# Two spectral attention layers on one core: sums and scalings that may run on ScalarE and GpSimd, an inverse transform written in runs of 16, second-layer statistics on ScalarE, and a new order of all units

## The chip, the cores and the metric

The kernel runs on one NeuronCore of a Trainium2 chip; the other cores hold nothing of it. The metric is the device time of one execution in microseconds (us), from the core's first instruction to its last. The core has TensorE (PE; its weight loads are shown apart as PEld), VectorE (DVE), ScalarE (ACT) and GpSimd (POOL); DMAs are issued from SyncE (SP) and ScalarE. SBUF is the on-chip memory, PSUM the memory that TensorE writes to.

## The reference

Two layers of the same form are applied to x of shape (2, 56, 128, 128), that is 2 batches of 56 images of 128 x 128. Cut to what matters, one layer is:

```python
def spectral_conv(x, w, b):              # 32 x 16 complex modes are kept
    xf = rfft2(x, norm='forward')
    top = einsum('bihw,iohw->bohw', xf[:, :, :16, :16], c(w[0]))
    bot = einsum('bihw,iohw->bohw', xf[:, :, -16:, :16], c(w[1]))
    ...
    return irfft2(of, s=(H, W), norm='forward') + b
def fno_layer(x, w, b, sw, sb, norm=False, act=False):
    y = spectral_conv(x, w, b)
    if norm: y = inorm(y)
    y = y + skip1x1(x, sw, sb)
    return gelu(y) if act else y
# layer, x: (2, 56, 128, 128)
xg = group_norm(x, 32)                   # groups over the last axis
xa = xg.reshape(112, 1, 128, 128); xn = inorm(xa)
k, q, v = (fno_layer(xn, ...) for each of K, Q, V)          # 8 heads each
attn = softmax(heads(q) @ heads(k).T * scale)               # 56 x 56 a head and batch
out = fno_layer(attn @ heads(v), P)
att = inorm(out + xa); an = inorm(att)
h = fno_layer(an, M0, norm=True, act=True)
h = fno_layer(h, M1, norm=True, act=False)
x = x + inorm(h) + att
```

## The kernel before

Everything is fp32. A batch's picture lies in SBUF as `X2[:, b]`, images on partitions (two halves of 64, 56 used) and 64 rows of 128 pixels along the free axis; it is worked on in 8 units of 128 x 1024, numbered n = 0 to 7. Transforms are matmuls with constant cosine and sine matrices, and only the 32 x 16 kept modes of an image are ever computed. The names of the steps stand in the code as functions, one call for each layer L and batch b:

- `turned`: transposes a unit on TensorE, copies it from PSUM to `P[b]`, and takes the sums for the group norm. Odd units do this on ScalarE with accumulating activations (a copy into `P`, then a square into `dump`); even units are copied and go through two `bn_stats` on VectorE.
- `modes_chain`, `gram`, `scores`, `values`, `softmax_chain`, `mix_chain`, `heads`, `norms_chain`: the group norm's scale, the forward transform, the attention in mode space, and the scale factors of all the instance norms. They are short dependent operations, mostly on VectorE; every inverse root (`root`) is one `pow` on GpSimd. `scale_x` multiplies the picture by the group norm's factor `gvr` in 16 pieces of 128 x 512, on GpSimd or VectorE.
- `gelu`, 8 units a batch: a unit's original picture is loaded from DRAM into one of three buffers `xr`; matmuls with the weights `BTx` mix the images into PSUM; VectorE reads that PSUM tile and `xr`, and writes their scaled sum to `X2` (the `scalar_tensor_tensor` X<-psum,scalars,xr); `synthesis` then adds the inverse transform to the same PSUM tile, which therefore has to wait for that read; ScalarE takes the gelu and a sum of squares, TensorE transposes and transforms the result.
- `h_chain`: the second transform's norms, short dependent operations again, ending with `inverse`, which makes `Z` by two VectorE transposes of 128 x 896 from PSUM.
- `end`, 8 units a batch: `synthesis` from `Z`, then P<-P,scalars,psum on VectorE, then the sum with `X2` (on GpSimd, on VectorE or, for odd units of layer 2, as a matmul with the identity), and a store to DRAM. In layer 1 the unit goes straight on to `turned` of layer 2.

In layer 1 batch 0 runs about 20 to 40 us ahead of batch 1, and layer 2 follows batch by batch. "Warm" matmuls (`psum<-xr,ones`) have no result that is used; 20 of them stand in the order.

All calls are recorded first as units (`Work`), each with the engines it may run on. `ORDER` then lists every unit by a step to its number and a letter for its engine (V VectorE, S ScalarE, G GpSimd, T TensorE, Q the SP queue), and `issue` gives them out in that order. `PLACES` names the PSUM bank of each tile. An engine does its instructions in the order in which they are issued; semaphores make it wait for others. All records of the trace carry the line of `issue`, so steps are told apart by tile names and shapes.

Of the kernel before, what the change touches and what calls it, by code (L numbers as in the profile page):

```python
# [11 lines left out]
ALU = mybir.AluOpType  # L12
# [9 lines left out]
11Q -2Q 17G 1G -17S -9Q -1S 2S 3S 23G 85G -78G 82V -1V -61T -16T -3V 15T -2T 1T 11T -19T 5T 10T -28G 89G -114Q 58S  # L22
-59Q 30G 5T 20S 6T -57S 112V 1G 1V 1T 2S -1S 3V -1S 10V -129Q 2Q 8Q -1Q 15G 38T -25T -3T 29S -6S -9T 11S -19T 81G -56T
-57Q 126V 3G 1G -10G -67V 5V 86V -145S 60V -7V 16T 75V -97V 23S -64S 56T 3T -2S 3S -20V 21V -6V 7V 79V -142Q 52S 7S
-45G 52S -43T 7T -4T 117V -109T -15T 16T 43T 66T -70T -69Q 66T 8S 45V -12G 15V 18V -24V 25G -71V -73Q 65T 86G -6V -75S
1S 81V -26T 2S 2S -3S 2S -132Q 156G -6T -81S -64S 111G -1G 62T 1S -29V 2V 1T 8T 1V -144V 140T 9T -3T -43V -6V 44V 1T
14V -134T 408S -369V 75V -76V 120G -1G -32V -2T 12S -104V 41G 68T -82V 79V -87T 1S 1V 76V 13T 1T -69G 12G -53V 359S
-255S -82T 1S -13S 123V -6G 227Q -304V -107V 197V -129T 4T -3V 1V 98T 1T 1T 49V -148V 2S 5V 27G 46T 3T 17T -178S 81S
81V 3S -77S 91T -16G 17V 97V -69T 3T 67V -73T -24V -17S 42V 3S -188T 258T -97T -194Q 9Q 442Q -256V 24T 17T -14T 70V
144Q -212S 580V -608V 41V -12T -85G 86T -87G 91T -3S 66G -96G -56G 662V -508V 510G -662G 157V -72T -30V 31T 3V -33T  # L30
32S -31S 39V 1S -227S 293T 1V 124S -122T -167G 70G 82V -88V 95G -17G -181G 697G -497T 1V -71T 79T -10V -61V 1T 63T 3T
-161V 87V 76V 9V -84S 8S 1T 7T 1T 1T 43T 1V -86V 109S -75S 68V -67T 1S 7T 1S -5T 73T 1S -68V 1V 1V 40T -88V 144G -43T
-63T 74S -23V -40T 62V -61S 1S 10S -22V 76T -11T 1V -43V -9V 55V -54V 62T 7V 15V -21T 1T 46T -169V 601V -599G 55T 67T
# [158 lines left out]
class Work:  # L192


    def __init__(self):
        self.units, self.open, self.note, self.taken = [], None, "", []
# [1017 lines left out]
```

## Time and profile before

| | |
|---|---|
| median of 3 runs | 419.46 us |
| lowest and highest run | 412.94 and 429.42 us |
| span of the profiled execution, first to last instruction | 416.2 us |
| instructions | 17307 |
| busy: PE, PEld, DVE, ACT, POOL | 350.4, 247.7, 310.3, 195.1, 200.1 us |

The profiled execution is a run of its own; no time is given around its span, which lies within the three timed runs and 0.8% under their median. A busy time counts the union of an engine's instructions, so TensorE's includes the warm matmuls.

### The profile page before, as it was taken

What the parts mean: (1) busy time and instruction counts of PE and PEld (TensorE: products, weight loads), DVE (VectorE), ACT (ScalarE), POOL (GpSimd) and SP (SyncE); (2) the same over time, 40 slices, a digit from 0 to 9 for tenths busy, and PEclk for the clock granted to TensorE, in tenths of its full rate; (3) what the DMA queues carried; (4) which work ended last, traced back from release to release, by engine and by line L of the source; (5) the groups of instructions that cost most, each with busy time, mean ns of one, the idle gap of its engine ahead of it and who ended that gap; (6) DMA issues with size and microseconds to landing.
All of it is one profiled execution on the core that took longest, in us unless ns stands there. A gap on an engine that the chain in (4) does not pass through costs nothing.

```text
span 416.2 us, 17307 instructions
## 1 busy us (share of the span) xinstructions
PE 350.4 (84%) x7812; PEld 247.7 (60%) x7812; DVE 310.3 (75%) x544; ACT 195.1 (47%) x307; POOL 200.1 (48%) x288
## 2 busy tenths in 40 slices
PE   6769969999759888498887999989899989899970
PEld 2435667688435576265774987858676544675440
DVE  1155898666768667997998799974898977489992
ACT  1246572333238762026698336832237877791000
POOL 4781095623999302215912589336487170013740
PEclk9898999989989999589968999999999998999995
DMA  6997831300014421133020101772245463300776
GB/s 205 226 246 137 189 89 27 49 3 5 3 44 114 92 76 41 30 99 96 3 70 23 48 27 46 182 219 66 60 123 157 113 157 89 91 4 24 236 239 212
DMA packets 15850, 41.19 MB, mean 99 GB/s; under 512 B 2432, under 2 KB 2816, under 8 KB 15744
## 3 DMA queue, kind: packets, MB, share of 16 engines
q1 hardware_dynamic: 8426, 21.52, 20.4%
q10 hardware_dynamic: 7350, 18.57, 16.2%
q8 instruction: 61, 1.00, 1.0%
q14 instruction: 13, 0.11, 0.1%
HBM read 25.40 MB, written 14.68 MB: 96 GB/s over the span
## 4 chain that ended last, share of the span: by engine, by line
PE 24%; DVE 22%; issue 5%; DMA 5%; ACT 4%; POOL 2%; ACTq 0%; SPq 0%; DVEq 0%; POOLq 0%
PE psum L222 24%; DVE P L222 9%; DVE X L222 3%; DMA xr<-store 3%; DVE WU L222 2%; ACT P L222 2%; DVE scalars L222 2%; DVE WB L222 1%; POOL X L222 1%; DMA store<-X 1%; DMA xr<-x 1%; ACT WB L222 1%; DVE stats L222 1%; ACT dump L222 1%; DVE vd L222 1%
## 5 line engine op out<-in xcount | busy, mean ns | idle before, releaser
L222 POOL TENSOR_TENSOR X<-X,gvr 128x512 f32<-128x512 f32 x47 | 61.0, 1324 | 33.1 <-DMA store<-X 17.1
L222 ACT COPY P<-psum 128x896 f32<-128x896 f32 (+5 forms) x47 | 34.4, 741 | 58.5 <-PE psum L222 53.1
L222 PE MATMUL psum<-C,P 56*128 56x56 f32 (+4 forms) x1124 | 50.1, 259 | 12.4 <-DVE X L222 10.5
L222 PE MATMUL psum<-P 128*56 128x56 f32 (+2 forms) x1600 | 56.9, 226 | 4.1 <-issue 4.0
L222 PEld LDWEIGHTS psum<-C,P 56*128 56x128 f32 (+4 forms) x1124 | 41.9, 166 | 27.9 <-DVE X L222 13.1
L222 POOL TENSOR_TENSOR scalars<-scalars 56x1 f32<-56x1 f32 (+2 forms) x24 | 14.8, 616 | 87.8 <-DVE scalars L222 87.8
L222 PEld LDWEIGHTS psum<-P 128*56 128x56 f32 (+1 forms) x1600 | 49.7, 136 | 8.6 <-issue 5.5
L222 DVE SCALAR_TENSOR_TENSOR X<-psum,scalars,xr 128x1024 f32<-128x1024 f32 x32 | 40.2, 1275 | 14.8 <-DMA xr<-store 4.9
L222 ACT ACTIVATE P<-psum,scalars 128x1024 f32<-128x1024 f32 x32 | 34.1, 1110 | 33.2 <-PE psum L222 33.1
L222 ACT ACTIVATE dump<-P 128x1024 fp8e4<-128x1024 f32 (+1 forms) x48 | 49.0, 1022 | 1.2 <-DVE X L222 0.5
L222 DVE SCALAR_TENSOR_TENSOR P<-P,scalars,psum 128x1024 f32<-128x1024 f32 x32 | 39.6, 1269 | 3.7 <-PE psum L222 3.7
L222 POOL TENSOR_TENSOR X<-P,X 128x512 f32<-128x512 f32 x25 | 33.5, 1367 | 16.2 <-DVE P L222 16.1
L222 PE MATMUL psum<-X,BTx 57*64 57x512 f32 x256 | 33.9, 624 | 1.2 <-DVE P L222 0.6
L222 PE MATMUL psum<-C,X 56*128 56x56 f32 x512 | 21.5, 232 | 8.6 <-DMA X<-x 7.1
L222 PEld LDWEIGHTS psum<-C,X 56*128 56x128 f32 x512 | 18.8, 144 | 15.1 <-DMA X<-x 8.1
L222 DVE STREAM_TRANSPOSE P<-psum 128x448 f32<-128x448 f32 (+1 forms) x24 | 23.8, 1002 | 4.9 <-PE psum L222 4.8
L222 PE MATMUL psum<-xr,ones 128*128 128x512 f32 x40 | 23.9, 742 | 2.2 <-POOL xr L222 1.9
L222 DVE COPY P<-psum 128x896 f32<-128x896 f32 (+4 forms) x25 | 21.2, 852 | 5.9 <-PE psum L222 5.5
L222 ACT ACTIVATE P<-psum 128x896 f32<-128x896 f32 x16 | 14.6, 912 | 20.0 <-PE psum L222 20.0
L222 PE MATMUL psum<-P,C 128*64 128x112 f32 (+2 forms) x200 | 19.3, 318 | 4.9 <-DVE P L222 4.4
L222 DVE BATCH_NORM_STATS2 stats<-P 128x6 f32<-128x448 f32 x32 | 18.4, 608 | 4.8 <-ACT P L222 4.7
L222 ACT COPY WB<-psum 128x896 f32<-128x896 f32 x21 | 18.8, 905 | 6.7 <-PE psum L222 6.2
(189 smaller groups left out, 654.3 us busy)
## 6 DMA issues: line engine op xcount, KB each, us to landing
X<-x SPq DMA_DIRECT2D x11, 448.0 KB
xr<-store SPq DMA_DIRECT2D x20, 224.0 KB
store<-X ACTq DMA_DIRECT2D x18, 224.0 KB
out<-P ACTq DMA_DIRECT2D x18, 224.0 KB
xr<-x SPq DMA_DIRECT2D x16, 224.0 KB
xr<-x ACTq DMA_DIRECT2D x16, 224.0 KB
store<-X SPq DMA_DIRECT2D x14, 224.0 KB
out<-P SPq DMA_DIRECT2D x14, 224.0 KB
```

The lines of the kernel that those rows point to most:

```text
L222: getattr(engines[letter], method)(*args, **kw)
```

## The change

Each recorded piece of work may now have alternatives: `either()`, `orelse()` and `decided()` bracket two or three ways to do it, and the order marks the units that are not issued with the letter X. The alternatives are:

- In `gelu`, the sum X<-psum,scalars,xr on VectorE, or a scaling from PSUM on ScalarE (X<-psum,scalars) and then a sum with `xr` on GpSimd (X<-X,xr, 128 x 1024). The order takes the second for 13 of 32 units.
- In `end`, as before; or P scaled on ScalarE (P<-P,scalars), summed with X on GpSimd (P<-P,X) ahead of the synthesis, and one VectorE sum with PSUM at the end; or, in layer 2, the sum with X by matmul. The order takes the second for 13 of 32 units and the matmul for 5 (8 before).
- In `prepare`, the tables WU and WT by tensor products on GpSimd or VectorE, or by small activations on ScalarE (one group of 16 of them is taken).
- Each warm matmul may be left out; 6 of 20 stay.

`inverse` turns its blocks into `Z` in runs of 16 neighbouring elements, where before each element went 64 elements (256 bytes) further; in return the weights that `synthesis` loads from `Z` lie 16 elements (64 bytes) apart, where before they were neighbours. The rows of the constant `gh` are reordered to match. In layer 2 all 8 units of `turned` take their sums on ScalarE; `bn_stats` and `bn_aggr` remain in layer 1. Engines, order and PSUM banks of all units are new.

```diff
 class Work:
+    def either(self):
+        self.groups.append([len(self.units)])
+    def orelse(self):
+        self.groups[-1].append(len(self.units))
+    def decided(self):
+        cuts = self.groups[-1] + [len(self.units)]
+        self.groups[-1] = [list(range(a, b)) for a, b in zip(cuts, cuts[1:])]
+    def left_out(self):
+        return self.letters.get(len(self.units)) == "X"
...
         for n, letter in order:
+            if letter == "X":
+                continue
...
 # _constants
-    v, r, a, e, c = j // 2, j % 2, idx // 8, idx // 2 % 4, idx % 2
+    v, r, a, e, c = j // 2, j % 2, idx // 4 % 4, idx % 4, idx // 16
...
 # build (and in the same way WT in prepare)
+                work.orelse()
+                for l0 in range(0, 16, 4):
+                    with work.unit():
+                        for l in range(l0, l0 + 4):
+                            S.activation(
+                                WUv[:, t0 : t0 + 4, :, 32 * h : 32 * h + 32]
+                                .rearrange("p t a (c l) -> p t a c l", c=2)[:, :, :, :, l],
+                                tcs[:, 0:16, t0 : t0 + 4].rearrange("p (a c) t -> p t a c", c=2),
+                                AF.Copy, scale=C["same"][:, 16 * h + l : 16 * h + l + 1],
+                            )
+                work.decided()
...
 # turned
-        if n % 2:
-            o = n - n % 2
+        if L == 1 or n % 2:
+            o = 2 * n if L == 1 else n - 1
...
 # inverse
-        Zv = Z.rearrange("p (h k) -> p h k", k=64)
+        Zv = Z.rearrange("p (c k q) -> p c k q", c=2, q=16)
...
-                Zv[:, :, i : i + 28].rearrange("p h i -> p i h"),
+                Zv[:, :, i : i + 28].rearrange("p c i q -> p i c q"),
...
 # modes_chain, L == 1
+            V.tensor_reduce(mv, totals.rearrange("p (n k) -> p k n", k=2), AX.X, ALU.add)
...
 # synthesis
-                    o = 64 * (8 * A + 2 * e)
+                    o = 4 * A + e
...
-                        lhsT=Z[32 * j : 32 * j + 32, o : o + N],
+                        lhsT=Z[32 * j : 32 * j + 32].rearrange("p (m q) -> p m q", q=16)[:, :, o],
...
 # gelu
+                work.either()
+                V.scalar_tensor_tensor(base, flat, cols[:, 1:2], xr[:, n % 3], ALU.mult, ALU.add)
+                work.orelse()
+                S.activation(base, flat, AF.Copy, scale=cols[:, 1:2])
+                tt("G", base, base, xr[:, n % 3], ALU.add)
+                work.decided()
...
 # end
+                S.activation(hold_[v], hold_[v], AF.Copy, scale=st["hs"])
+                tt("G", hold_[v], hold_[v], bases[v], ALU.add)
...
+                V.scalar_tensor_tensor(h3, h3, st["hs"], flat[v], ALU.mult, ALU.add)
+                m = 512 if L == 0 else 1024
+                for o in range(0, 1024, m):
+                    tt("GV", dst[:, o : o + m], h3[:, o : o + m], base[:, o : o + m], ALU.add)
+                V.tensor_tensor(dst, flat[v], h3, ALU.add)
+                k = opened[v]
+                if L == 0:
+                    work.groups.append([[first, first + 1, first + 2], [k, k + 1, first + 3]])
+                else:
+                    work.groups.append([[first, first + 1], [k, k + 1, first + 2], [k + 2, first]])
...
 # warm
+        work.either()
         p = bank()
         T.matmul(p, lhsT=ones, rhs=xr[:, 0, :512], start=True, stop=True)
+        work.orelse()
+        work.decided()
...
 ORDER = """
-11Q -2Q 17G 1G -17S -9Q -1S 2S 3S 23G 85G -78G 82V -1V -61T -16T -3V 15T -2T 1T 11T -19T 5T 10T -28G 89G -114Q 58S
+33G -22S 15V 2G 27T -4T -10X 15X -24G -3G -19Q 103V -104S 107G 1V 1G 1V -5V 6V 1V -121S 1Q 114G -113S 47X 12T 61T -60S
```

What the new order does is shown at three places. The first is TensorE at the end of batch 0's load: transposes of units (`C,X`), warm matmuls (`xr,ones`), and the matmul that sums the group norm's statistics (`scalars,C 128x2`). Before:

```order
L222 MATMUL psum_63<-C_64,X2_68 128x56 x16
L222 MATMUL psum_63<-xr_78,ones_80 128x512 x4
L222 MATMUL psum_63<-C_64,X2_68 128x56 x64
L222 MATMUL psum_63<-xr_78,ones_80 128x512 x6
L222 MATMUL psum_63<-C_64,X2_68 128x56 x16
L222 MATMUL psum_63<-scalars_81,C_64 128x2
L222 MATMUL psum_63<-C_64,X2_68 128x56 x48
L222 MATMUL psum_63<-stage_65,C_64 32x5x8 x32
L222 MATMUL psum_63<-C_64,scalars_81 1x32
```

With the change:

```order
L247 MATMUL psum_63<-C_64,X2_68 128x56 x80
L247 MATMUL psum_63<-xr_78,ones_80 128x512 x2
L247 MATMUL psum_63<-C_64,X2_68 128x56 x32
L247 MATMUL psum_63<-stage_65,C_64 32x5x8 x32
L247 MATMUL psum_63<-xr_78,ones_80 128x512
L247 MATMUL psum_63<-scalars_81,C_64 128x2
L247 MATMUL psum_63<-C_64,X2_68 128x56 x32
L247 MATMUL psum_63<-P0_69,fwg0_96 32x448 x16
L247 MATMUL psum_63<-C_64,scalars_81 1x32
```

One warm matmul stands ahead of the statistics' matmul where six stood, and the transform (`P,fwg`) follows with fewer transposes of batch 1 between.

The second place is VectorE where batch 0 of layer 1 goes over from `norms_chain` to `gelu`: the inverse's two transposes, the multiplications of batch 1's picture (`X<-X,gvr1`), and the first sums of `gelu` (X<-psum,scalars,xr). Before:

```order
L222 STREAM_TRANSPOSE P0_69<-psum_63 128x28x32 x2
L222 TENSOR_TENSOR X2_68<-X2_68,gvr1_100 128x512
L222 SCALAR_TENSOR_TENSOR X2_68<-psum_63,scalars_81,xr_78 128x1024 x2
L222 TENSOR_SCALAR vd1_101<-C_64,scalars_81 56x56
L222 TENSOR_TENSOR dcq0_98<-psum_63,P0_69 1x56
L222 TENSOR_SCALAR dcq0_98<-dcq0_98,der0_92 1x56
L222 TENSOR_TENSOR D0_84<-D0_84,psum_63 128x448
L222 STREAM_TRANSPOSE stage_65<-stage_65 128x128
L222 SCALAR_TENSOR_TENSOR X2_68<-psum_63,scalars_81,xr_78 128x1024
```

With the change:

```order
L247 TENSOR_TENSOR D0_84<-D0_84,psum_63 128x448
L247 TENSOR_TENSOR X2_68<-X2_68,gvr1_102 128x512
L247 COPY scalars_81<-psum_63 128x2
L247 STREAM_TRANSPOSE P0_69<-psum_63 128x28x2x16 x2
L247 SCALAR_TENSOR_TENSOR X2_68<-psum_63,scalars_81,xr_78 128x1024 x2
L247 TENSOR_TENSOR X2_68<-X2_68,gvr1_102 128x512 x2
L247 SCALAR_TENSOR_TENSOR vd1_103<-psum_63,C_64 56x56
L247 TENSOR_REDUCE scalars_81<-vd1_103 56x1
L247 TENSOR_SCALAR scalars_81<-scalars_81 56x1
```

The multiplication that stood between the transposes and the first two sums now stands ahead of the transposes, and two more follow the sums.

The third place is ScalarE in layer 2, where `gelu` goes over from batch 0 (`P0`) to batch 1 (`P1`): gelus (P<-psum,scalars), squares (into `dump`), copies for the transform (`WB`) and loads of `xr`. Before:

```order
L222 ACTIVATE P0_69<-psum_63,scalars_81 128x1024 x2
L222 DMA xr_78<-store_79 56x1024
L222 COPY WB_74<-psum_63 128x896
L222 ACTIVATE dump_75,scalars_81<-P0_69 128x1024
L222 COPY WB_74<-psum_63 128x896
L222 ACTIVATE P1_70<-psum_63,scalars_81 128x1024 x2
L222 DMA xr_78<-store_79 56x1024
L222 ACTIVATE dump_75,scalars_81<-P0_69 128x1024
L222 ACTIVATE P1_70<-psum_63,scalars_81 128x1024 x2
```

With the change:

```order
L247 DMA xr_78<-store_79 56x1024
L247 ACTIVATE dump_75,scalars_81<-P0_69 128x1024 x2
L247 COPY WB_74<-psum_63 128x896
L247 ACTIVATE dump_75,scalars_81<-P0_69 128x1024
L247 ACTIVATE X2_68<-psum_63,scalars_81 128x1024
L247 ACTIVATE dump_75,scalars_81<-P0_69 128x1024
L247 DMA xr_78<-store_79 56x1024
L247 ACTIVATE P1_70<-psum_63,scalars_81 128x1024 x2
L247 ACTIVATE X2_68<-psum_63,scalars_81 128x1024
L247 DMA xr_78<-store_79 56x1024
```

Two scalings of a unit's sum (X<-psum,scalars), of batch 1's units 1 and 3, now stand between ScalarE's gelus and squares, and where two copies stood, one stands.

## Rows read from the trace of the kernel before

**Rows 1.** The page: busy times; shares of the chain that ended last

```profile
PE 350.4 (84%) x7812; PEld 247.7 (60%) x7812; DVE 310.3 (75%) x544; ACT 195.1 (47%) x307; POOL 200.1 (48%) x288
...
PE 24%; DVE 22%; issue 5%; DMA 5%; ACT 4%; POOL 2%; ACTq 0%; SPq 0%; DVEq 0%; POOLq 0%
```

**Rows 2.** Stretches of 20 or 8 us: PE, PEld, DVE, ACT, POOL busy (x); PEclk; DMA

```profile
24.00:32.00 8.00, 4.18 (x68) 3.04 (x67) 4.20 (x8) 2.34 (x5) 5.72 (x18) 0.88 1.02 243
...
160.00:180.00 20.00, 13.36 (x119) 9.06 (x116) 17.13 (x46) 1.81 (x5) 5.76 (x10) 0.66 0.23 59
...
200.00:220.00 20.00, 16.32 (x430) 13.54 (x424) 18.59 (x27) 17.83 (x31) 8.89 (x7) 0.83 0.14 38
```

**Rows 3.** Timeline, 30 to 39 us: start us, us, instructions merged

```profile
30.87 6.68 PE L222 MATMUL psum<-xr,ones 128*128 128x512 f32 x12
...
35.68 0.16 DVE L222 SCALAR_TENSOR_TENSOR scalars<-scalars 128x2 f32<-128x2 f32 x1
...
38.12 0.38 PE L222 MATMUL psum<-scalars,C 128*128 128x2 f32 x2
```

**Rows 4.** Timeline, 110 to 120 us

```profile
110.32 6.34 DVE L222 TENSOR_TENSOR X<-X,gvr 128x512 f32<-128x512 f32 x1
...
110.89 4.94 POOL L222 TENSOR_TENSOR X<-X,gvr 128x512 f32<-128x512 f32 x4
...
119.10 2.09 PE L222 MATMUL psum<-C,P 32*128 32x128 f32 x32 [5.74 <-DVE X L222]
```

**Rows 5.** VectorE's groups by form: busy us, mean ns, idle before

```profile
L222 DVE SCALAR_TENSOR_TENSOR X<-psum,scalars,xr 128x1024 f32<-128x1024 f32 x32 | 40.2, 1275 | 14.8 <-DMA xr<-store 4.9 <-DMA xr<-x 4.1 <-ACT P L222 3.2
...
L222 DVE BATCH_NORM_STATS2 stats<-P 128x6 f32<-128x448 f32 x32 | 18.4, 608 | 4.8 <-ACT P L222 4.7
L222 DVE TENSOR_TENSOR X<-X,gvr 128x512 f32<-128x512 f32 x17 | 18.2, 1074 | 0.3 <-DMA xr<-x 0.3
L222 DVE STREAM_TRANSPOSE P<-psum 128x896 f32<-128x896 f32 x8 | 13.7, 1732 | 2.6 <-PE psum L222 2.5
...
L222 DVE STREAM_TRANSPOSE P<-psum 128x448 f32<-128x448 f32 x16 | 10.1, 637 | 2.3 <-PE psum L222 2.3
```

**Rows 6.** ScalarE's groups by form

```profile
L222 ACT ACTIVATE P<-psum,scalars 128x1024 f32<-128x1024 f32 x32 | 34.1, 1110 | 33.2 <-PE psum L222 33.1
...
L222 ACT ACTIVATE dump<-P 128x896 fp8e4<-128x896 f32 x16 | 15.2, 949 | 0.2
L222 ACT ACTIVATE P<-psum 128x896 f32<-128x896 f32 x16 | 14.6, 912 | 20.0 <-PE psum L222 20.0
...
L222 ACT ACTIVATION_READ_ACCUMULATOR dump<-P 128x1 f32 x48 | 9.2, 192 | 0.0
```

**Rows 7.** GpSimd's groups by form

```profile
L222 POOL TENSOR_TENSOR X<-P,X 128x512 f32<-128x512 f32 x25 | 33.5, 1367 | 16.2 <-DVE P L222 16.1
...
L222 POOL TENSOR_TENSOR P<-P,X 128x1024 f32<-128x1024 f32 x6 | 14.1, 2357 | 14.8 <-DVE P L222 14.8
```

**Rows 8.** Chain in time, 160 to 185 us and 320 to 366 us

```profile
167.66 1.28 DVE X L222
...
174.29 1.08 DVE X L222
...
334.57 6.45 DMA xr<-store
...
353.61 4.76 DMA xr<-store
```

**Rows 9.** Timeline at 361 us: one synthesis of 16 matmuls

```profile
361.26 0.98 PEld L222 LDWEIGHTS psum<-C,P 32*128 32x128 f32 x32 [0.95 <-DVE X L222]
361.26 1.17 PE L222 MATMUL psum<-C,P 32*128 32x128 f32 x32 [0.82 <-DVE X L222]
```

**Rows 10.** TensorE's groups by form: rows*columns of the array, mean ns

```profile
L222 PE MATMUL psum<-X,BTx 57*64 57x512 f32 x256 | 33.9, 624 | 1.2 <-DVE P L222 0.6 <-ACT P L222 0.4
...
L222 PE MATMUL psum<-P,fwg 128*32 128x448 f32 x128 | 14.3, 576 | 1.6 <-DVE P L222 1.5
```

More of the change, by code (lines that the diff above doesn't have):

```diff
@@ L192, with __init__ @@
 class Work:
-    def __init__(self):
+    def __init__(self, order):
         self.units, self.open, self.note, self.taken = [], None, "", []
+        self.groups, self.letters = [], dict(order)
+    def either(self):
[7 more added lines that the diff above has]
+        return self.letters.get(len(self.units)) == "X"
     def call(self, choices):
@@ L243, in fno_layers @@
     nc = tc.nc
-    work = Work()
+    work = Work(decoded(ORDER))
     V, S, G, T = (Engine(work, c) for c in "VSGT")
@@ L1089, in end @@
             both = [pair(), pair()]
-            summed = [L == 1 and v == 1 for v in range(2)]
+            flat = [t.rearrange("p r m -> p (r m)") for t in both]
+            bases = [X2[:, b, 8 * n : 8 * n + 8, :].rearrange("p e w -> p (e w)") for n in (2 * A, 2 * A + 1)]
+            hold_ = [unit_of(P[b], n) for n in (2 * A, 2 * A + 1)]
+            dsts = bases if L == 0 else hold_
+            opened, fresh = [], []
             for v in range(2):
@@ L1093, in end @@
                 work.note = f"end{L}{b}.{n}a"
-                if summed[v]:
+                first = len(work.units)
+                S.activation(hold_[v], hold_[v], AF.Copy, scale=st["hs"])
+                tt("G", hold_[v], hold_[v], bases[v], ALU.add)
+                if L == 1:
+                    fresh.append(work.left_out())
                     with work.unit():
@@ L1103, in end @@
                                 )
+                else:
+                    fresh.append(True)
+                opened.append(first)
             work.note = f"end{L}{b}.{2 * A}s"
-            synthesis(A, both, st["Z"], [not k for k in summed])
+            synthesis(A, both, st["Z"], fresh)
             for v in range(2):
@@ L1123, in fno_layers @@
     for _ in range(20):
+        work.either()
         p = bank()
         T.matmul(p, lhsT=ones, rhs=xr[:, 0, :512], start=True, stop=True)
+        work.orelse()
+        work.decided()
     prs, st = [None, None], [[{}, {}], [{}, {}]]
-    stats = [(hold(f"stats{b}", [N, 8, 6]), hold(f"totals{b}", [N, 8])) for b in range(B)]
+    stats = [(hold(f"stats{b}", [N, 8, 6]), hold(f"totals{b}", [N, 16])) for b in range(B)]
     for b in range(B):
```

171 lines of the change are left out of this document (90 added, 81 removed).

## The prediction

> **What bounds the kernel now.** I read the page first. TensorE is busy 84% of the span and VectorE 75%, ScalarE and GpSimd under half [rows 1]; on the chain that ended last TensorE has 24% and VectorE 22%, the rest goes to issue, DMA and many short links [rows 1]. So no engine alone sets the end: TensorE works nearly without pause, and where it pauses, VectorE is mostly what it waited for. A cut on VectorE pays only where TensorE waits; a cut on TensorE pays only where its queue has no slack behind it. The stretches come next: in 160 to 180 us TensorE was busy 13.36 of 20 us at a mean granted clock of 0.66, VectorE 17.13, ScalarE 1.81; in 200 to 220 us the clock was 0.83 [rows 2]. Ahead of the statistics' matmul lie warm matmuls [rows 3]; in 110 to 120 us TensorE stood 5.74 us for one VectorE multiplication [rows 4]. The groups give the price of one instruction on each engine [rows 5 to 7], the chain in time the waits that count [rows 8].
>
> **The change part by part.** The sum is made against the profiled span, 416.2 us, which lies 0.8% under the median; at the end it is multiplied by 419.46/416.2 = 1.008.
>
> Warm matmuls. Of 20, 6 stay. The statistics were ready at 35.68 + 0.16 = 35.84 us, their matmul ran at 38.12, behind a block of warm records that began at 30.87 [rows 3]. With one warm unit in front of it in place of six, the 2.28 us shrink to about 0.1: **-2.2**. It is on the path, since the group norm's factor, the multiplications and the transform all follow from it. The bound is 0 if the last statistics come later themselves (odd units' sums are ScalarE's), and the other warm matmuls stand where TensorE waits for loads: 0. What they cover is the clock: 24 to 32 us had 4.18 us of TensorE work and 0.88 granted [rows 2]; with less work there the clock may drop, which I take as 0, since that stretch was half idle already and nearly kept it.
>
> The multiplication. One VectorE X<-X,gvr of mean 1074 ns [rows 5] took 6.34 us, from 110.32 on, while four of GpSimd's ran in 4.94 us from 110.89 on [rows 4]: an excess of 6.34 - 1.07 = 5.27 us, and TensorE's synthesis stood 5.74 us for it. It now stands ahead of the transposes, the first sums directly behind them. I take the excess less one normal multiplication ahead of the transposes, 5.27 - 1.07: **-4.2**. The bounds are -5.7, and +5.3 if one of the now 33 multiplications on VectorE (17 before) is held up as long at a place where TensorE waits.
> What the rows show is that two ordinary instructions side by side cost one of them five times its mean. [...]
>
> The inverse's transposes. 16 of 128 x 896 at 1732 ns (8 of them go to P, the rest to tables); the transposes of 128 x 448 write neighbours and take 637, two of them 1274 [rows 5]. I take that as the new price, the nearest row: 0.458 us less for each, 16 x 0.458 = 7.3 us of VectorE. They make Z, twice for each of 8 passages. I count about 5 of the 16 on the chain (a pair where batch 0 goes over to `gelu`, a pair where the second does, one near the end), the others beside TensorE work: 5 x 0.458 = **-2.3**, bounds 0 (the price is in reading PSUM and stays) and -7.3.
>
> The price of that on TensorE, weights for the synthesis loaded 16 elements apart, is shown by no row. Before, the 32 loads of a synthesis took 0.98 us beside 1.17 us of matmuls [rows 9], so they are covered as long as they stay under 1.17. The nearest row is a moving operand that jumps after every 14 elements: 448 columns in 576 ns, 1.29 ns a column, against 624/512 = 1.22 unbroken [rows 10], 5% more. I take 0, since 0.98 x 1.05 is still covered; the ends are 0 and VectorE's own factor 1732/1274 = 1.36: 0.98 x 1.36 = 1.33, 0.16 us over, for 32 units +5.
>
> Two sums at the passage into `gelu`. The chain from the second batch's norms through 167.66 to 174.29 us holds two VectorE sums of 1.28 and 1.08 us [rows 8]. Two of 13 sums that are now a scaling on ScalarE, which is busy 1.81 of 20 us there [rows 2]: **-2.4**; bounds 0 (the order puts another VectorE instruction in their place) and -2.4.
>
> Waits for `xr`. VectorE stood 4.9 + 4.1 = 9.0 us before its 32 sums for loads of `xr` [rows 5]; on the chain such loads stand at 334.57 (6.45 us) and 353.61 (4.76) [rows 8]. With 13 sums moved to ScalarE and GpSimd, VectorE no longer stands there, and what waits is GpSimd, off the path: 9.0 x 13/32 = **-3.7**, bounds 0 and -9.0.
>
> Layer-2 statistics. 16 bn_stats of 608 ns leave VectorE [rows 5], 9.7 us; ScalarE gets 8 times a copy and a square with their readings, 912 + 949 + 2 x 192 = 2.24 us [rows 6], 18 us, and 13 scalings of at most a gelu's 1110 ns [rows 6], 14 us: 195 + 33 = 228 of 416 us, no bound as a sum. In place it is closer: in 200 to 220 us ScalarE was at 17.83 [rows 2]. 0, bounds -2.6 (about four bn_stats at chain ends) and +3 (one and a half such pairs queued ahead of a gelu).
>
> GpSimd. Its sums grow from 128 x 512 at 1367 ns to 128 x 1024 at 2357 [rows 7]: per element no dearer, but a `pow` of a norm waits for a longer one, (2.36 - 1.37)/2 = 0.5 us more on average, for six roots in the norm and `h` chains beside such sums **+3**, bounds 0 and +6. The three identity sums fewer (5 units in place of 8), the tables' alternatives and the loads moved on SP's queue lie under other work: 0; their cover is TensorE at work without pause from 55 us on.
>
> Sum: -2.2 - 4.2 - 2.3 - 2.4 - 3.7 + 3 = -11.8; 416.2 - 11.8 = 404.4, times 1.008 is **408 us**. Its terms' bounds, few of which fall the same way, make it 399 to 411.
>
> **Rivals.** [...]
>
> (b) The same as before. A sum in two steps frees its `xr` buffer 1.11 + 2.36 - 1.28 = 2.2 us later [rows 5 to 7], and there are three buffers: where 7 of 32 loads were late, 13 x 2.2 x 7/32 = +6.3, and the -3.7 is lost: 404.4 + 10 = 414.4, 418 us. For it: loads of `xr` are on the chain already [rows 8]. Against: the scalings go before `xr` arrives, so PSUM comes free early and the synthesis need not wait.
>
> (c) Slower: the weights. If loads 64 bytes apart take twice as long, 1.96 us for a synthesis against 1.17, each is 0.79 us longer, and 32 of them +25: 429.7 x 1.008 = 433 us. It makes the kernel slower than I can tell from no change when a synthesis gets 0.63 us longer, at 1.8 times the load's time. For it: VectorE's transposes do get dearer with scattered elements, 1732 against 1274 [rows 5]. Against: the 5% of the scattered moving operand [rows 10]; at 1.36 times it costs 5 us, and the forecast holds.
> [...]
>
> **How the numbers follow.** Forecast 0.50, (a) 0.13, (b) 0.25, (c) 0.12, with what else could slow it. A measurement can tell about 2% from no change (three runs spread from 412.94 to 429.42), so the bounds are 411.1 and 427.9 us. Faster: 0.50 + 0.13 = 0.63; same 0.25; slower 0.12. The range leaves (c) out, and (a)'s far end: its lower end is 397 less what is left of the `xr` waits, 9.0 - 3.7 = 5.3, so 391; its upper end is (b) with +5 for the loads, 423.
>
> **What will show it.** Warm: the statistics' matmul starts within 0.3 us of its statistics. Multiplication: no VectorE X<-X,gvr over 2 us ahead of the first synthesis of batch 0. Transposes: their mean near 1.28 us; if near 1.73, that term is 0. Weights: PEld of a synthesis near 0.98 us and its matmuls 1.17; 1.4 or more for the loads speaks for (c). Waits: VectorE's idle time for `xr` under 6 us; if GpSimd's X<-X,xr waits for loads and gelus wait for GpSimd, (b). [...] I would be wrong most likely where a term that I put off the path, above all ScalarE's added 33 us or GpSimd's long sums, holds TensorE in layer 2.

## The result: 9% slower, and the profile after

The changed kernel took 453.53 us (median of 4 runs, 451.42 to 456.29) against 417.5 us before in the same comparison: a ratio of 1.0917, 95% interval 1.0798 to 1.1037. That is 36 us more where 12 us less were forecast, and outside the stated range. The profiled execution spans 454.4 us (416.2 before). Where some runs of a kernel were in a slower state of the chip, its ratio is taken from the others, while a time given alone is the median of all its runs.

The page of the changed kernel: busy times, the granted clock by slice, and the shares of the chain that ended last.

```profile
PE 377.6 (83%) x7760; PEld 280.4 (62%) x7760; DVE 320.8 (71%) x581; ACT 229.9 (51%) x360; POOL 213.9 (47%) x235
...
PEclk9998698998999986899799959988799799998875
...
PE 54%; DVE 18%; POOL 9%; DMA 9%; issue 6%; ACT 2%; POOLq 1%; ACTq 0%; DVEq 0%
```

Against [rows 1], TensorE's busy time has grown by 27 us although 14 warm matmuls are gone, and its share of the chain from 24% to 54%: the changed kernel is held by TensorE more than by any other engine. The granted clock, 0.938 on average over the span before, is 0.894.

TensorE's weight loads and matmuls of the synthesis and VectorE's transposes, by form (busy us, mean ns, idle before). Two of the groups before:

```profile
L222 PEld LDWEIGHTS psum<-C,P 32*128 32x128 f32 x512 | 17.9, 194 | 14.1 <-DVE X L222 13.1 <-issue 0.4 <-POOL X L222 0.2
...
L222 PE MATMUL psum<-C,P 32*128 32x128 f32 x512 | 21.6, 294 | 10.6 <-DVE X L222 10.5
```

With the change:

```profile
L247 PEld LDWEIGHTS psum<-C,P 32*128 32x128 f32 x512 | 31.4, 304 | 3.6 <-issue 1.6 <-DVE X L247 1.1 <-DVE WT L247 0.4
L247 PEld LDWEIGHTS psum<-C,WB 32*128 32x128 f32 x256 | 15.0, 305 | 6.1 <-DVE P L247 2.9 <-issue 2.8 <-ACT P L247 0.3
L247 PEld LDWEIGHTS psum<-C,WT 32*128 32x128 f32 x256 | 14.9, 305 | 4.2 <-issue 2.4 <-ACT P L247 1.4 <-DVE scalars L247 0.3
...
L247 PE MATMUL psum<-C,P 32*128 32x128 f32 x512 | 34.7, 391 | 1.0 <-issue 0.9 <-DVE X L247 0.2
...
L247 DVE STREAM_TRANSPOSE P<-psum 128x896 f32<-128x896 f32 x8 | 8.8, 1106 | 4.4 <-PE psum L247 4.4
```

In the trace of before the same three groups of loads took 17.9 + 8.1 + 8.5 = 34.5 us at 186 to 194 ns; now 61.3 us at 304 to 305. Their matmuls went from 41.0 to 67.4 us (34.7 here, 16.5 and 16.2 for WB and WT), +26.4. One synthesis in the timeline, to hold against [rows 9]:

```profile
428.56 1.87 PEld L247 LDWEIGHTS psum<-C,WB 32*128 32x128 f32 x32 [2.14 <-issue]
...
428.59 2.13 PE L247 MATMUL psum<-C,WB 32*128 32x128 f32 x32 [1.82 <-DVE WB L247]
```

1.87 and 2.13 us where 0.98 and 1.17 stood: nearly what rival (c) assumed for the loads (1.96). The transposes did fall, from 1732 [rows 5] to 1106 ns, further than the 1274 that was taken.

The second place is the head. SP's and ScalarE's DMA issues and TensorE's first transposes, in the timeline of 0 to 60 us:

```profile
0.74 0.40 SPq L247 DMA_DIRECT2D stage<-weights  x1
1.18 0.97 ACTq L247 DMA_DIRECT2D C<-const_all  x2
...
13.23 0.35 PE L247 MATMUL psum<-C,X 56*128 56x56 f32 x1 [7.68 <-DMA C<-const_all]
17.56 13.72 SPq L247 DMA_DIRECT2D X<-x  x4
...
36.73 0.32 ACTq L247 DMA_DIRECT2D X<-x  x1
...
38.21 0.38 PE L247 MATMUL psum<-scalars,C 128*128 128x2 f32 x2 [0.34 <-DVE gc L247]
...
42.11 0.34 ACTq L247 DMA_DIRECT2D X<-x  x1
...
53.24 1.10 PE L247 MATMUL psum<-C,X 56*128 56x56 f32 x16 [7.65 <-DMA X<-x]
```

The first two loads of constants now both go out on ScalarE's queue, and the first weights ahead of x on SP's: the first transpose waits 7.68 us for the constants and starts at 13.23 us (11.84 before). ScalarE issues its last two loads of x at 36.73 and 42.11 us, since they stand in its order behind work that itself waits for earlier loads; the transposes of batch 1 wait 7.65 us for a load of x, until 53.24. The statistics' matmul runs at 38.21, as late as in [rows 3].

The third place is layer 2, batch 1. VectorE beside GpSimd in the timeline:

```profile
314.11 4.92 POOL L247 TENSOR_TENSOR X<-X,gvr 128x512 f32<-128x512 f32 x4
314.17 4.91 DVE L247 TENSOR_SCALAR vd<-C,scalars 56x56 f32<-56x56 f32 x1 [0.53 <-POOL scalars L247]
...
413.99 2.35 POOL L247 TENSOR_TENSOR P<-P,X 128x1024 f32<-128x1024 f32 x1 [0.51 <-ACT P L247]
...
414.23 2.16 DVE L247 TENSOR_SCALAR WU<-C,scalars,sm 56x56 f32<-56x56 f32 x1
416.30 2.36 POOL L247 TENSOR_TENSOR X<-X,xr 128x1024 f32<-128x1024 f32 x1
416.31 2.39 DVE L247 TENSOR_SCALAR WU<-C,scalars 56x56 f32<-56x56 f32 x1
...
418.75 0.76 PE L247 MATMUL psum<-WU,ones 56*128 56x112 f32 x2 [2.96 <-DVE WU L247]
...
419.33 7.37 POOL L247 TENSOR_TENSOR P<-P,X 128x1024 f32<-128x1024 f32 x3 [0.67 <-ACT P L247]
...
420.34 1.26 DVE L247 SCALAR_TENSOR_TENSOR P<-P,scalars,psum 128x1024 f32<-128x1024 f32 x1
...
422.20 2.22 DVE L247 TENSOR_SCALAR WU<-WU,C 128x56 f32<-128x56 f32 x1
```

A scaling of 56 x 56 constants, `vd<-C,scalars`, takes 4.91 us beside four of GpSimd's multiplications, and ends when they end. At the tail three operations of 0.3 us (293 to 360 ns before) take 2.2 to 2.4 us, each beside sums of GpSimd of 2.36 us, and TensorE waits 2.96 us for the result; P<-P,scalars,psum, which reads PSUM as well, takes its usual 1.26 us beside the same sums. It is the hold-up of [rows 4], in other places. One thing differs: at the tail the first operation ends at 416.39, as GpSimd goes over from one sum to the next (416.30), while `vd<-C,scalars` stood through all four multiplications.

The stretches of [rows 2], which hold other work in the longer kernel, and 40 to 60 us; the first line is that of before:

```profile
40.00:60.00 20.00, 17.13 (x467) 13.17 (x463) 16.87 (x32) 12.98 (x23) 10.03 (x13) 1.00 0.73 158
```

```profile
40.00:60.00 20.00, 12.35 (x202) 8.71 (x199) 9.66 (x16) 8.61 (x20) 10.22 (x10) 0.66 0.62 109
...
160.00:180.00 20.00, 16.61 (x290) 11.97 (x292) 16.02 (x45) 7.42 (x13) 8.59 (x8) 0.77 0.14 37
...
200.00:220.00 20.00, 18.23 (x312) 14.40 (x312) 13.80 (x14) 16.98 (x31) 15.24 (x10) 0.88 0.35 99
```

The clock is a little better in these two stretches (0.77 and 0.88 for 0.66 and 0.83), and has a new low in the late head, 0.66 for 1.00 in 40 to 60 us, where TensorE was busy 12.35 of 20 us. What part of the 36 us the lower clock is, no run separates; the four runs of e6 below had means from 0.899 to 0.932 and lie about 2 us apart.

### The profile page after: what moved, and what is told of

The parts are those of the page before. It is cut to its first block, busy times and chain, and to the rows that moved or that the text cites. A ratio compares the mean times of both kernels' runs of the same rounds, so it can differ in the third digit from the quotient of the medians.

```text
span 454.4 us, 17234 instructions
## 1 busy us (share of the span) xinstructions
PE 377.6 (83%) x7760; PEld 280.4 (62%) x7760; DVE 320.8 (71%) x581; ACT 229.9 (51%) x360; POOL 213.9 (47%) x235
## 4 chain that ended last, share of the span: by engine, by line
PE 54%; DVE 18%; POOL 9%; DMA 9%; issue 6%; ACT 2%; POOLq 1%; ACTq 0%; DVEq 0%
PE psum L247 54%; DMA X<-x 9%; DVE P L247 9%; POOL X L247 4%; DVE WU L247 4%; POOL stage L247 2%; ACT P L247 2%; POOL scalars L247 1%; DVE vd L247 1%; POOL P L247 1%; DVE WB L247 1%; DVE X L247 1%; DVE scalars L247 1%; DVE psum L247 1%; POOLq L1281 1%
## 5 line engine op out<-in xcount | busy, mean ns | idle before, releaser
L247 PEld LDWEIGHTS psum<-C,P 56*128 56x128 f32 (+4 forms) x1124 | 56.9, 219 | 16.5 <-issue 6.8
L247 POOL TENSOR_TENSOR X<-X,xr 128x1024 f32<-128x1024 f32 x13 | 30.8, 2371 | 42.5 <-ACT X L247 42.5
L247 POOL TENSOR_TENSOR P<-P,X 128x1024 f32<-128x1024 f32 x15 | 35.6, 2393 | 23.2 <-DVE P L247 18.7
L247 PEld LDWEIGHTS psum<-C,X 56*128 56x128 f32 x512 | 22.0, 164 | 35.7 <-DMA X<-x 10.3
L247 POOL TENSOR_TENSOR X<-X,gvr 128x512 f32<-128x512 f32 x31 | 40.7, 1329 | 3.4 <-DVE gvr L247 3.4
L247 ACT ACTIVATE P<-P,scalars 128x1024 f32<-128x1024 f32 (+1 forms) x19 | 25.6, 1373 | 10.8 <-DVE scalars L247 7.4
L247 DVE SCALAR_TENSOR_TENSOR P<-P,scalars,psum 128x1024 f32<-128x1024 f32 x19 | 24.0, 1269 | 9.3 <-PE psum L247 8.3
L247 DVE SCALAR_TENSOR_TENSOR X<-psum,scalars,xr 128x1024 f32<-128x1024 f32 x19 | 24.1, 1279 | 6.9 <-PE psum L247 6.6
L247 POOL TENSOR_TENSOR X<-P,X 128x512 f32<-128x512 f32 x11 | 16.6, 1514 | 23.1 <-DVE P L247 23.0
L247 DVE COPY WB<-psum 128x896 f32<-128x896 f32 x19 | 20.4, 1085 | 9.7 <-PE psum L247 8.9
L247 DVE TENSOR_TENSOR X<-X,gvr 128x512 f32<-128x512 f32 x33 | 26.1, 818 | 0.0
```

The lines of the kernel that those rows point to most:

```text
L247: getattr(engines[letter], method)(*args, **kw)
```

## The experiments

Theory A: the 64-byte spacing of the synthesis weights costs the time, on TensorE's path. Theory B: it is the order, its head and the hold-ups between GpSimd and VectorE. Ratios are to the kernel before in the same comparison; a difference in us between two comparisons is less sure than one within a comparison, by some us.

**The layout alone, in both orders.** The layout of Z is set by one number q, the length of the runs: the weights of a synthesis lie q elements apart. Between the kernels only the index of `gh`, the view of Z and the weights' slice differ, here from runs of 16 to runs of 2:

```diff
-    v, r, a, e, c = j // 2, j % 2, idx // 4 % 4, idx % 4, idx // 16
+    v, r, a, e, c = j // 2, j % 2, idx // 8, idx // 4 % 2 * 2 + idx % 2, idx // 2 % 2
...
-        Zv = Z.rearrange("p (c k q) -> p c k q", c=2, q=16)
+        Zv = Z.rearrange("p (c k q) -> p c k q", k=64, q=2)
...
-                    o = 4 * A + e
+                    o = 256 * A + e // 2 * 128
...
-                        lhsT=Z[32 * j : 32 * j + 32].rearrange("p (m q) -> p m q", q=16)[:, :, o],
+                        lhsT=Z[32 * j : 32 * j + 32].rearrange("p (m q) -> p m q", q=2)[:, o : o + N, e % 2],
```

The changed order with the old layout (q = 1):

> The changed kernel with Z laid out as before (weights of the synthesis neighbours, transposes scattered). Theory A (the strided weight loads sit on TensorE's path): the 1024 loads go from 305 ns back to about 190, TensorE gets 26 us of its 378 back, the 16 transposes cost 10 us more on VectorE, of which 2 to 5 show: 428 to 435 us. [...]

437.41 us, ratio 1.0534 (1.0441 to 1.0627): 16 us less than the changed kernel, and still 20 more than before. Both theories hold a part.

The old order with runs of 16:

> The kernel before with only the inverse in runs of 16. Theory A: 32 synthesis units 0.83 us longer each, +26, less 2 to 10 for transposes of 1.1 in place of 1.73 us: 434 to 442 us. Theory B: 410 to 420 us.

426.45 us, 1.026 (1.0151 to 1.0369): the layout alone makes the old kernel slower, though by less than theory A's sum.

Runs of 4 (16 bytes) and of 2 (8 bytes), weights 4 and 2 elements apart, in the old order:

> The kernel before with the inverse in runs of 4 (16 bytes), weights 4 elements apart. [...] Theory A with a price that grows with the distance: loads near 200 ns, 408 to 418 us. Theory B: 410 to 420 us.

> [...] Theory B: 410 to 420 us.

Runs of 4: 432.39 us, 1.0374 (1.0278 to 1.047). Runs of 2: 413.98 us, 0.9932 (0.9883 to 0.998). The loads and transposes by form, runs of 16, of 4 and of 2, one fence each:

```profile
L222 PEld LDWEIGHTS psum<-C,P 32*128 32x128 f32 x512 | 30.9, 305 | 4.2 <-DVE X L222 3.1 <-issue 0.5 <-POOL X L222 0.2
...
L222 DVE STREAM_TRANSPOSE P<-psum 128x896 f32<-128x896 f32 x8 | 8.7, 1097 | 3.2 <-PE psum L222 2.5 <-ACT P L222 0.7
```

```profile
L222 PEld LDWEIGHTS psum<-C,P 32*128 32x128 f32 x512 | 33.1, 322 | 10.5 <-DVE X L222 9.4 <-issue 0.7
...
L222 DVE STREAM_TRANSPOSE P<-psum 128x896 f32<-128x896 f32 x8 | 8.7, 1096 | 2.8 <-PE psum L222 2.0 <-ACT P L222 0.7
```

```profile
L222 PEld LDWEIGHTS psum<-C,P 32*128 32x128 f32 x512 | 19.6, 211 | 7.7 <-DVE X L222 6.5 <-issue 0.5 <-POOL X L222 0.2
...
L222 DVE STREAM_TRANSPOSE P<-psum 128x896 f32<-128x896 f32 x8 | 8.7, 1094 | 2.5 <-PE psum L222 1.8 <-ACT P L222 0.7
```

The price does not grow steadily with the distance: neighbours took 194 ns, elements 8 bytes apart 211, 16 bytes apart 322 and 64 bytes apart 305. Why it steps up between 8 and 16 bytes was not shown. The transposes are as short with runs of 2 (1094 ns) as with 16 (1097). Runs of 2 keep all of the transposes' gain for at most a tenth of the loads' price (36.9 us for the 1024 loads, 61.4 with runs of 16, 34.5 with neighbours); in the changed order they cost nothing that the trace shows, 35.7 us in e5 below against 37.0 with neighbours in e1.

**The rest of the change, with runs of 2.**

> The changed kernel with runs of 2 in place of runs of 16 (weights 2 elements apart), all else as changed. From the old layout in the new order (437 us) the 16 transposes give back 16 x 0.62 = 10 us of VectorE. If about the same part of it shows as in the old order (3 of 10): 434 us; if TensorE waits for all of it: 427 us. Loads near 200 ns, transposes near 1.1 us.

435.23 us, 1.037 (1.0276 to 1.0463). Runs of 16 in place of 2 cost 453.53 - 435.23 = 18.3 us in the changed order, 426.45 - 413.98 = 12.5 in the old one (23 and 14 us by the ratios), where the loads grew by nearly as much (24.5 us by the trace, against 25.6): less of it shows there. What remains, 17 us over before, belongs to the rest of the change. The head and layer 2 were then taken one at a time and together.

The head: the loads' letters and places at the start of the order are those of before.

```diff
-33G -22S 15V 2G 27T -4T -10X 15X -24G -3G -19Q 103V -104S 107G 1V 1G 1V -5V 6V 1V -121S 1Q 114G -113S 47X 12T 61T -60S
+10S -10S 2S 3S 6Q -2Q -8Q 3Q -1Q 3Q 2Q 8Q -1Q -1Q 4Q 2Q -3Q -5Q 21G -7V 2G 27T -4T -10X 15X -24G -3G 84V 3G 1V 1G 1V
```

> As e5_new_order_runs_of_2, but the loads of x, the first constants and the first weights are given to the queues in the sequence of the kernel before (11 of 16 loads of x on SP in a row, ahead of the rest). Theory H (the head loses 8 to 12 us because ScalarE issues late loads behind its squares, and all of layer 1 follows from it): TensorE's gap of 10 us ahead of batch 1's transposes goes, the first Gram matmuls come 8 us earlier, 6 to 10 us less than e5. Rival (the head's lag is made up in layer 1, and layer 2 is held elsewhere): within 3 us of e5.

424.64 us, 1.0138 (1.0065 to 1.0212), 10.6 less than e5, a little more than theory H's 6 to 10. TensorE's timeline:

```profile
11.79 1.28 PE L248 MATMUL psum<-C,X 56*128 56x56 f32 x16 [6.23 <-DMA X<-x]
...
29.69 0.38 PE L248 MATMUL psum<-scalars,C 128*128 128x2 f32 x2 [0.34 <-DVE gc L248]
...
48.99 1.74 PE L248 MATMUL psum<-C,X 56*128 56x56 f32 x27 [6.00 <-issue]
```

The statistics' matmul has come from 38.21 to 29.69 us, the gap ahead of batch 1's transposes ends at 48.99 in place of 53.24.

Layer 2: 28 units get the letter V for G, and the sum may run there.

```diff
-                tt("G", hold_[v], hold_[v], bases[v], ALU.add)
+                tt("GV", hold_[v], hold_[v], bases[v], ALU.add)
```

> As e5_new_order_runs_of_2, but 28 units of layer 2 (the multiplications X<-X,gvr and the sums P<-P,X of end) go from GpSimd to VectorE at the same places of the order. Theory C (GpSimd's long runs hold up VectorE's short operations that read SBUF, on the chain): the constants' scalings vd<-C,scalars fall from 4.9 to under 1 us, the tail's WU<-C,scalars from 2.2 to 0.3, 8 to 18 us less than e5 although VectorE gets some 25 us more work. Rival (the hold-ups lie beside TensorE's work, VectorE is the bound): 0 to 10 us more than e5.

423.04 us, 1.0134 (1.0081 to 1.0186), 12.2 less than e5, though VectorE got the work.

> Both edits, head loads as before and layer 2's sums on VectorE. If both theories hold and add: 14 to 28 us under e5, 403 to 418 us, level with the kernel before or under it. If one falls, the size of the other.

411.93 us, 0.9828 (0.9755 to 0.9902): 23.3 less than e5; the two add (10.6 + 12.2 = 22.8), and the kernel is faster than the changed one and, by 1 to 2.5%, than the one before. VectorE's short scalings by form, of the changed kernel and of this one:

```profile
L247 DVE TENSOR_SCALAR vd<-C,scalars 56x56 f32<-56x56 f32 x4 | 9.3, 2328 | 1.5 <-POOL scalars L247 1.5
L247 DVE TENSOR_SCALAR P<-xf 1x56 f32<-1x56 f32 x3 | 7.6, 2523 | 0.0
...
L247 DVE TENSOR_SCALAR WU<-C,scalars 56x56 f32<-56x56 f32 x4 | 3.3, 820 | 0.0
```

```profile
L248 DVE TENSOR_SCALAR vd<-C,scalars 56x56 f32<-56x56 f32 x4 | 4.3, 1063 | 1.5 <-POOL scalars L248 1.5
L248 DVE TENSOR_SCALAR P<-xf 1x56 f32<-1x56 f32 x3 | 2.7, 899 | 0.0
...
L248 DVE TENSOR_SCALAR WU<-C,scalars 56x56 f32<-56x56 f32 x4 | 1.2, 295 | 0.0
```

2328, 2523 and 820 ns have become 1063, 899 and 295: most of layer 2's hold-ups are gone. Some remain in it, beside GpSimd's other work: `vd<-C,scalars` takes 2.36 us at 240.72 beside a sum of layer 1's `end`, and a scaling P<-C,scalars,der 2.37 us at 319.65 beside a sum of `gelu`; so do those of layer 1.

**Which part of layer 2, and whether layer 1 as well.** First e6 with the 19 multiplications alone:

> As e6_head_loads_as_before (424.6 us), with only the 19 multiplications X<-X,gvr of layer 2 moved from GpSimd to VectorE, the 9 sums of end left on GpSimd. If the hold-up in the attention chain at 290 to 310 us (4.9 + 4.9 us) and the one in the tail (four times 2 us) count alike: 417 to 419 us, half of e8's gain. If the tail alone counts: 424 us. If the attention chain alone: 412 us.

417.44 us, 0.9986 (0.9943 to 1.0029): 7.2 of the 12.7 us between e6 and e8 come from the multiplications, 5.5 from the 9 sums of `end`; by the ratios (1.0138, 0.9986, 0.9828) each has half. In its trace vd<-C,scalars is down to 1067 ns, while the tail's WU<-C,scalars still takes 819. Then e8 with the 29 units of layer 1 moved too:

> As e8_both, with layer 1's multiplications and sums of end (29 units more) on VectorE too. If GpSimd holds up VectorE on the path in layer 1 as well: 400 to 408 us. If there VectorE is the bound (up to 29 us more work for it): 412 to 425 us.

418.49 us, 1.0057 (1.0022 to 1.0093): 6.6 us worse than e8. vd<-C,scalars takes 280 ns there, so its hold-ups are gone, and yet the time is longer, with 335.2 us of work on VectorE (324.6 in e8). Moving everything is no rule.

**The weights' price in the repaired order,** e8 with runs of 16:

> As e8_both (411.9 us), with the runs of 16 of the change. If the weight loads' price is on TensorE's path in any order: 18 us more than e8 as between e5 and the changed kernel, 428 to 432 us. If it showed there only since the order was held elsewhere too, or part is covered as in the old order (12 us between runs of 16 and of 2): 420 to 425 us.

426.11 us (420.06 to 429.08), 1.0169 (1.0061 to 1.0277), 14.2 us more than e8, nearer to the second of the two figures expected: part of the price is covered, as in the old order. Runs of 16 alone turn a kernel that is faster than before into one that is slower.

**The sums of `gelu` back on VectorE,** e8 with the 13 sums in one instruction again, at the place in the order where the scaling stood, as in this unit (its old sum 1V for 1X, its scaling and its GpSimd sum X):

```diff
-123Q -5T 7V -95T 89X 1S 460V -706G 233T 1S -107T 1S 29T -18V 113X 2T 1S -88V -29G 109G -79S 70T 1V 429T -510T 2S
+123Q -5T 7V -95T 90X -1V 461V -706G 233T 1S -107T 1S 29T -18V 113X 2T 1S -88V -29G 109X -79S 70T 1V 429T -510T 2S
```

> As e8_both, with the 13 sums of gelu that the change gave to ScalarE and GpSimd back on VectorE in one instruction. By the prediction's steps (waits for xr -3.7, two sums off the passage into gelu -2.4, GpSimd's cost +3) the way back costs 3 us: 414 to 418 us. If the two-step sums hold up VectorE and free xr late (rival b), the way back gains: 404 to 410 us.

439.55 us (433.16 to 445.06); even its fastest run lies 20 us above the slowest of e8 (412.77). VectorE's sums and TensorE's matmuls of the synthesis by form, of e12 and of e8:

```profile
L248 DVE SCALAR_TENSOR_TENSOR X<-psum,scalars,xr 128x1024 f32<-128x1024 f32 x32 | 40.3, 1275 | 19.4 <-PE psum L248 14.7 <-DMA xr<-x 2.5 <-issue 2.2
...
L248 PE MATMUL psum<-C,P 32*128 32x128 f32 x512 | 25.9, 312 | 12.0 <-DVE X L248 10.7 <-DVE scalars L248 1.2
```

```profile
L248 DVE SCALAR_TENSOR_TENSOR X<-psum,scalars,xr 128x1024 f32<-128x1024 f32 x19 | 23.9, 1268 | 7.1 <-PE psum L248 4.9 <-DMA xr<-x 2.1
...
L248 PE MATMUL psum<-C,P 32*128 32x128 f32 x512 | 22.2, 299 | 1.2 <-DVE X L248 1.2
```

The two-step sums gain here, far more than the 3 us expected of the way back, and hardly through `xr`: VectorE waits 2.5 us for it in e12 and 2.1 in e8. TensorE's synthesis, which adds to the PSUM tile that the sum reads, stands 10.7 us for VectorE's sums in e12 and 1.2 in e8; it stood 10.5 us in the kernel before and 0.2 in the changed one. VectorE in turn stands 14.7 us for TensorE's matmuls ahead of these sums (4.9 in e8), with everything behind them in its queue. How much of the loss an order made for these sums would win back stays open.

**What in the head.** e5 with the first six transfers as before, and e5 with the later loads alone:

> As e5_new_order_runs_of_2 (435.2 us), with only the first six transfers as before: first constants on SP, first weights on ScalarE's queue; the later loads of x stay as changed. If the late start of the constants (7.8 us of waiting, first transposes at 13.4 and 17.7 in place of 11.8 us) costs the 10.6 us that e6 gave back: 425 us. If the late loads of batch 1 cost them: 433 to 436 us.

> As e5_new_order_runs_of_2, with the first transfers as changed and only the later loads of x as before: 11 of 16 in a row on SP, two early and three later on ScalarE's queue. If the loads that ScalarE issues behind its squares are the cause: 424 to 427 us. If the start is: 433 to 436 us.

431.28 us, 1.0354 (1.0294 to 1.0414), and 425.43 us (four runs, 417.65 to 428.88, so no interval). By the medians the late loads count for 9.8 of the 10.6 us and the start for 4. They overlap, and e14's runs lie 11 us apart: that the late loads are the larger part is likely, their size is not shown.

**The held-up multiplication in the old order.** The kernel before, with the VectorE multiplication of [rows 4] moved behind the next short operations:

```diff
--13V 83V -4V 5T -231G 161T 84T -104G -10V -57V 1V 173Q -11S
+70V -4V 5T -231G 161T 84T -104G -10V -57V 1V 72V 101Q -11S
```

> The kernel before with one VectorE multiplication, the one of 6.34 us, moved from ahead of the first two sums of gelu to behind the next short operations of VectorE. By the prediction's term: 4.2 us less than before, 413 to 415 us. If what is late there is set by something else, or the hold-up falls on the next operation that reads SBUF: within 1.5 us of before.

411.48 us, 0.985 (0.9798 to 0.9902): 5.8 us less for one instruction. The timeline at the place:

```profile
106.57 2.48 DVE L223 SCALAR_TENSOR_TENSOR X<-psum,scalars,xr 128x1024 f32<-128x1024 f32 x2 [0.27 <-PE psum L223]
106.74 4.96 POOL L223 TENSOR_TENSOR X<-X,gvr 128x512 f32<-128x512 f32 x4
108.96 3.07 DVE L223 TENSOR_SCALAR vd<-C,scalars 56x56 f32<-56x56 f32 x1
109.10 0.98 PEld L223 LDWEIGHTS psum<-C,P 32*128 32x128 f32 x32 [0.33 <-DVE X L223]
```

The two sums now follow the transposes at once, and the synthesis with them; GpSimd's run holds up `vd<-C,scalars` in the multiplication's place, 3.07 us, and TensorE has other work meanwhile.

> The kernel before with the two single edits that gained: runs of 2 (e4, -0.7%) and the one multiplication moved (e15, -1.5%). If they add: 0.978 of before, 407 to 410 us, under e8_both. If the second takes what the first gave: 411 to 412 us.

412.61 us, 0.9921 (0.9882 to 0.9961): the two don't add. The trace of e4 shows why: with transposes of 1.1 us the multiplication ran in 0.65 us at 107.93, ahead of GpSimd's run from 108.98, so that the hold-up that e15 removes was no longer there in e4; `vd<-C,scalars` was held up for 4.13 us in its place. e8 and e15 are the fastest, within each other's intervals.

## Why the prediction was wrong, point by point

**The weights: the term that failed.** "I take 0, since 0.98 x 1.05 is still covered": the 5% were taken from the moving operand that jumps after every 14 elements [rows 10], as the nearest row; its runs of 56 bytes say nothing of loads in which every element lies 64 bytes from the last. Between runs of 16 and of 2, whose transposes take the same time, the term measured 12.5 to 18.3 us (14 to 23 by the ratios). VectorE's factor, put down as the upper end (1.36, +5), was too small for an end, too: the loads took 1.6 times as long, and TensorE's matmuls grew by as much as they (26.4 beside 26.8 us). Rival (c), whose factor of two was an assumption, had the place, the sum of a synthesis's loads (1.96 us expected, 1.87 measured) and the side; 0.12 was too little for the one cost of the change that no row of before bounded. Its +25 is close to what the trace's loads and matmuls grew by, of which only a part shows in the time; its 433 us left out the other two places.

**The head: a term put at 0.** "[...] the loads moved on SP's queue lie under other work: 0; their cover is TensorE at work without pause from 55 us on" looked at SP's later loads and left out those before 55 us, where TensorE itself waits for loads (7.65 us in the trace). It measured 10.6 us: seven loads of x on ScalarE's queue, five before, the last of them behind its squares. ScalarE's queue was not looked at.

**GpSimd beside VectorE: mis-sized.** +3 was taken for GpSimd's longer instructions, through the waits of the norms' `pow`. The runs gave 12.2 us in layer 2, by the hold-up of the multiplication term, whose upper bound of +5.3 named the case "at a place where TensorE waits", for one place; there were at least five in layer 2 of the changed kernel (5.06 us at 298.03 and 4.91 at 314.17 the longest).

**The multiplication (-4.2): right in the old order.** By itself it gave 5.8 us there (e15), a little more than the term, whose price of 1.07 us for a normal one contained the held-up one; the other 16 take (18.2 - 6.34)/16 = 0.74 us. In the changed order the first sums do follow the transposes, but a GpSimd run now holds up a scaling P<-C,scalars,der in the same passage, 3.42 us from 104.91 on where 0.30 is usual. What the move gains there was not tried alone.

**Warm matmuls (-2.2): right in mechanism, not in effect.** The statistics were ready at 37.99 + 0.16 = 38.15 us, their matmul ran at 38.21; the wait is gone, but the statistics came 2.3 us later, through the loads. With the head mended they are at 29.69. That the clock would not suffer from their leaving in 24 to 32 us holds for this execution (1.00), but not for that of e5, whose head is the same: 0.59 there, and 0.66 in 40 to 60 us. Rival (a), the clock, fell, and no run shows the 397 us that the range's lower end is worked out from: the granted clock was 0.77 in 160 to 180 us and 0.88 in 200 to 220 us (0.66 and 0.83 before), and the changed kernel took 453.5 us.

**The transposes (-2.3):** 1.10 us in place of the 1.28 taken, 16 x 0.63 = 10 us less on VectorE; in the old order, runs of 2 gave 3 us, and nothing more once the multiplication was moved (e16 against e15).

**Waits for `xr` and the sums at the passage (-3.7 and -2.4):** the idle time before VectorE's sums for loads of `xr` went from 9.0 us [rows 5] to 0.4:

```profile
L247 DVE SCALAR_TENSOR_TENSOR X<-psum,scalars,xr 128x1024 f32<-128x1024 f32 x19 | 24.1, 1279 | 6.9 <-PE psum L247 6.6 <-DMA xr<-store 0.4
...
L247 POOL TENSOR_TENSOR X<-X,xr 128x1024 f32<-128x1024 f32 x13 | 30.8, 2371 | 42.5 <-ACT X L247 42.5
```

GpSimd never waits for `xr` here, only for ScalarE, so rival (b) fell. But e12 waits only 2.5 us for `xr` with all sums on VectorE, so most of that fall is not the two-step sums'. What they remove is TensorE's wait for VectorE's sums, 10.5 us before and 0.2 here; the prediction has it only as a reason against (b) ("the synthesis need not wait"), not as a term. The layer-2 statistics (0) were not tried alone.

The sum from the runs: 453.5 changed; -18.3 by runs of 2, -10.6 by the head's loads, -12.7 by layer 2's units on VectorE, 411.9 us. Against the old order with runs of 2 (413.98) that leaves 2 us of gain from all the rest (4 by the ratios), where 12 were forecast, and three costs lay on top of it.

## What to carry to other kernels

A layout that spares one engine a scattered write can hand the scatter to the engine that reads it (here transposes from 1732 to 1106 ns, weight loads from 194 to 304); a price that no row bounds is first measured alone, and a middle layout may keep both sides cheap (two fp32 neighbours: 1094 and 211 ns in the old order). When work moves to GpSimd, look for short VectorE operations on SBUF beside its long runs, and at what waits for them: here steps of 0.3 us took 2.2 to 4.9 us each. When a DMA is issued from a computing engine's queue, look at the work ahead of it there: ScalarE's load of x went out at 36.73 us here, behind a square that started at 36.72. This was in the head, where that work waits for loads itself, and giving the head's loads the places of before gave back 10.6 us.

## What the runs showed of the hardware

Weight loads of 32 x 128 fp32 took 194 ns from neighbours (the kernel before), 191 to 211 with elements 8 bytes apart (e5, e4), 322 at 16 (e3) and 305 at 64 bytes (e2); a transpose of 128 x 896 into runs of 8 bytes was as fast (1094 ns, e4) as into 64 bytes (1106, the changed kernel), while single elements 256 bytes apart took 1732 (the kernel before).

A VectorE operation with one SBUF tensor and no PSUM operand (vd<-C,scalars) stood from the start of GpSimd's run of four multiplications to its end, 4.91 beside 4.92 us, and not for one of them; P<-P,scalars,psum, with a PSUM operand, kept its 1.26 us beside GpSimd's sums, and a scaling of one column (scalars<-scalars,der, 56x1, at 414.10) its 0.20 us. How long such a hold-up lasts is not settled: in these four multiplications VectorE did not get in between two instructions of GpSimd, while at the tail WU<-C,scalars,sm ended at 416.39, between two sums that follow one another without a pause.
